# A four-layer graph network on one core: own-group scores in layer 2 formed once and transposed, and both halves of 20 rows in one block in layer 1

## The chip, the cores and the metric

The kernel runs on one core of one Trainium2 chip. The metric is the device time of one execution in microseconds (us). The core has a matrix engine (TensorE, PE in the profile; its weight loads are PEld), a vector engine (VectorE, DVE), an engine for functions of one argument (ScalarE, ACT), a general engine (GpSimd, POOL), an engine that mostly issues transfers (SyncE, SP), and DMA engines that move data between memory (HBM) and the on-chip buffer. TensorE writes its products to a small accumulator memory, PSUM, cut into banks (`BANK = 512` fp32 columns in the code).

## The reference

Four graph layers run one after the other on the same features `x` (2708 x 512) and the same 0/1 adjacency matrix `adj` (2708 x 2708, about 1.2% ones, with ones on the diagonal). Each layer is wrapped in a residual and a normalisation, `x = layernorm(x + layer(x))`. Layers 1 and 2 are the ones the change touches:

```python
def layer1(x, adj, W, b):
    A = (adj != 0).astype(x.dtype)
    hidden = x @ W + b
    deg = jnp.sum(A, axis=0)
    return A @ hidden / deg[:, None]

def layer2(x, adj, weight, bias, node_w, edge_w):
    node_att = softmax(x @ node_w, axis=0)
    h = x @ edge_w
    e = h @ h.T                       # symmetric, 2708 x 2708
    e = jnp.where(adj > 0, e, NEG_BIG)
    edge_att = softmax(e, axis=1)
    support = x @ weight
    return adj * (node_att * edge_att) @ support + bias
```

Layer 0 is a two-pass attention with batch norms and small MLPs, layer 3 a plain attention with `adj` added twice to its scores. Everything is in fp32.

## The kernel before

The 2708 nodes are cut into `NT = 22` blocks: 21 of 128 rows and a last one of `REST = 20`. The 512 features are `C = 4` chunks of 128. The program is written as a sequence of tile operations; a planner decides the order of the instructions on each engine from the order of the program and from its own estimate of when each operand is ready, and it places the semaphores. So work of neighbouring steps is interleaved on an engine, and no order is written out by hand. Each engine then executes its own list in order. Transfers issued by SP (loads) and by POOL (stores and small moves) have a queue each.

**Layer 1** (lines 859 to 967). `hidden` is formed block by block and split into two tiles of the reduced format fp32r, `hid_hi` (rounded) and `hid_lo` (the rest), so that two single-pass products together keep the precision (lines 909 to 915). Both tiles have 22 blocks; the rows 20 to 127 of the last one are zeroed at the start by two DVE memsets (lines 867 and 868). The neighbour sum (lines 924 to 958) takes the rows of the output in groups of four blocks, six groups in all (the last has two). For each block `jt` of keys, SP loads the matching part of the transposed adjacency into `raw` (five buffers), DVE turns it into 0/1 in `at` (three buffers), and PE multiplies it, for each of the group's blocks, with `hid_hi[:, jt, :]` and then `hid_lo[:, jt, :]`, adding up in one PSUM bank per output block. For the last `jt`, `raw` is zeroed first and only 20 rows are loaded.

**Layers 2 and 3** share one function, `softmax_layer` (line 1022). Queries go in seven groups (`GROUPS`) of three blocks, 384 columns; the last group has a fourth block of 20, 404 columns. Layer 2 runs from about 1697 us of the span to 2400. For each group and each of the 22 blocks of keys, `one_score` (line 1086) forms a 128 x 384 block of scores in one of two PSUM banks (`ps_s`), masks it with the adjacency (`masked`: an ACT instruction on the loaded `a_cols`, then a DVE instruction that reads the bank), and takes the running maximum on DVE. When a group is through, `spread_max` (line 1138) turns the column maxima. 25 steps behind the scores, `one_sum` (line 1174) subtracts the maximum (DVE), takes the exponential (ACT), adds to the row sums and multiplies by the adjacency (DVE), and multiplies with the values on PE (line 1195). So the scores of one group run together with the sums of the group before it; in the first group there are only scores, and after the last only sums.

In layer 2 the scores are symmetric, and the kernel uses that between groups (`mirror=True`): a block whose keys belong to a later group is copied from its bank by ACT into `s_raw` (three buffers, tag `sraw`), stored by POOL (lines 1123 to 1126), and later loaded back by SP (`load_kept`) and transposed by PE into the bank (lines 1092 to 1098) in place of being formed again. Blocks whose keys lie in the group itself are formed in full (lines 1099 to 1107): four fp32 matmuls over the chunks of features, each of the full width of the group. `key_order` (line 1031) spreads the blocks that are loaded back evenly among the others. In groups 0 to 4 the three own blocks are among the first of those that are formed, so they stand near the start of the group; in groups 5 and 6 they are spread more widely.

An fp32 matmul is two instructions in the profile, an fp32r matmul or a transposition one.

Of the kernel before, what the change touches and what calls it, by code (L numbers as in the profile page):

```python
# [8 lines left out]
F32 = mybir.dt.float32  # L9
# [8 lines left out]
P = 128  # L18
# [11 lines left out]
def gnn_stack_kernel(  # L30
# [25 lines left out]
    nc = tc.nc  # L56
# [3 lines left out]
    NT = (N + P - 1) // P  # L60
    NFULL = N // P
# [4 lines left out]
    Q = 32  # L66
    REST = N - NFULL * P
# [6 lines left out]
    ident = const.tile([P, P], F32, name="ident")  # L74
# [81 lines left out]
    with ExitStack() as l0:  # L156
# [326 lines left out]
        with (  # L483
# [82 lines left out]
            half = C // 2  # L566
            raws = []
            for name, w in (("wq", wq), ("wk", wk)):
                for part in range(2):
                    tag = "z" if len(raws) == 3 else "a"  # L570
# [21 lines left out]
        with (  # L592
# [18 lines left out]
            for c in range(C):  # L611
                ps = psum.tile([P, F], F32, tag="misc", name="ps_m", bufs=2)
                for o in range(C):
# [5 lines left out]
                        stop=(o == C - 1),  # L619
# [9 lines left out]
            for ci, (c0, w) in enumerate(CHUNKS):  # L629
                pss = []  # L630
                for o in range(C):
# [3 lines left out]
                    ps = pair[:, o % HP, :]  # L635
                    for c in range(C):
# [5 lines left out]
                            stop=(c == C - 1),  # L642
# [12 lines left out]
                for o in range(C):  # L655
                    dst = ft[:, o, c0 : c0 + w]
                    r = elu(
                        att, pss[o][:, :w], w, bias[:, 0, o : o + 1], bias[:, 1, o : o + 1]
                    )
# [4 lines left out]
                while turned < NT and sum(BLOCKS[turned]) <= c0 + w:  # L664
                    j0, n = BLOCKS[turned]
# [193 lines left out]
    with (  # L859
        tc.tile_pool(name="l1", bufs=1) as p1,  # L860
        tc.tile_pool(name="l1ps", bufs=2, space=PSUM) as psum,
        ExitStack() as main,
    ):
        hid_hi = p1.tile([P, NT, F], F32R, name="hid_hi")
        hid_lo = p1.tile([P, NT, F], F32R, name="hid_lo")
        if NFULL < NT:
            nc.vector.memset(hid_hi[:, NFULL, :].bitcast(F32), 0.0)
            nc.vector.memset(hid_lo[:, NFULL, :].bitcast(F32), 0.0)

        work = main.enter_context(tc.tile_pool(name="l1w", bufs=2))
        with tc.tile_pool(name="l1a", bufs=1) as pre:
            b1_sb = load_row(pre, b1, "b1_sb")
            w1_sb = pre.tile([P, C, F], F32, name="w1_sb")
            nc.vector.tensor_copy(w1_sb, w1_held)
            for ci in range(len(early), NCH):
                load_x(ci)
            turned = 0  # L880
            for ci, (c0, w) in enumerate(CHUNKS):
                for c in range(C):
                    cols = ot[:, c, c0 : c0 + w]
                    nc.scalar.activation(
                        cols,
                        cols,
                        AF.Identity,
                        bias=shift3[:, c : c + 1],
                        scale=scale3[:, c : c + 1],
                    )  # L890
                    nc.vector.tensor_tensor(cols, cols, x_held[ci][:, c, :], ALU.add)
                while turned < NT and sum(BLOCKS[turned]) <= c0 + w:
                    it = turned
                    i0, n = BLOCKS[it]
                    tp = psum.tile([P, C, P], F32, tag="po0", name="tp_out")
                    for c in range(C):
                        nc.tensor.transpose(tp[:n, c, :], ot[:, c, i0 : i0 + n], ident)
                    ps = psum.tile([P, F], F32, tag="po1", name="ps_hid")
                    project_rows(ps, ot[:, :, i0 : i0 + n], w1_sb, n)
                    rows = tp[:n].rearrange("p c d -> p (c d)")  # L900
                    mean, rstd = row_stats(rows, n)
                    less = small.tile([P, 1], F32, tag="less", name="less")
                    nc.vector.tensor_scalar(less[:n], mean, rstd, -1.0, ALU.mult, ALU.mult)
                    nc.scalar.activation(xs[:n, it, :], rows, AF.Identity, bias=less[:n], scale=rstd)
                    full = pre.tile([P, F], F32, tag="full", name="full")
                    nc.vector.scalar_tensor_tensor(
                        full[:n], ps[:n], rstd, b1_sb[:n], ALU.mult, ALU.add
                    )
                    nc.scalar.copy(hid_hi[:n, it, :], full[:n])
                    nc.vector.tensor_tensor(  # L910
                        hid_lo[:n, it, :],
                        full[:n],
                        hid_hi[:n, it, :].bitcast(F32),
                        ALU.subtract,
                    )
                    turned += 1

        feats.close()
        l2_weights = ExitStack()
        pw2 = l2_weights.enter_context(tc.tile_pool(name="l2wt", bufs=1, side="right"))  # L920

        G = 4
        later = []
        for g in range(0, NT, G):
            group = range(g, min(g + G, NT))
            c0 = g * P
            w = min(N, c0 + G * P) - c0
            if g == G:
                ew_sb = load_weight(pw2, edge_w, "ew_sb")
                w2_sb = load_weight(pw2, w2, "w2_sb")  # L930
                nw_sb = load_row(pw2, node_w, "nw_sb")
                b2_sb = load_row(pw2, b2, "b2_sb")
            pos = {
                it: psum.tile([P, F], F32, tag=f"po{it - g}", name="ps_nb", bufs=1 + (it - g < 2))
                for it in group
            }
            for jt, (j0, m) in enumerate(BLOCKS):
                if later and jt % 4 == 3:
                    y, n = later.pop(0)
                    layer_norm(y, y, n)  # L940
                raw = work.tile([P, G * P], F32, tag="raw", name="raw", bufs=5)
                a = work.tile([P, G * P], F32R, tag="at", name="at", bufs=3)
                if m < P or w < len(group) * P:
                    nc.vector.memset(raw[:, : len(group) * P], 0.0)
                nc.sync.dma_start(raw[:m, :w], adjT[j0 : j0 + m, c0 : c0 + w])
                nc.vector.tensor_scalar(  # L946
                    a[:, : len(group) * P], raw[:, : len(group) * P], 0.0, None, ALU.not_equal
                )
                for it in group:
                    at = a[:, (it - g) * P : (it - g + 1) * P]  # L950
                    for k, half in enumerate((hid_hi, hid_lo)):
                        nc.tensor.matmul(  # L952
                            pos[it],
                            at,
                            half[:, jt, :],
                            start=(jt == 0 and k == 0),
                            stop=(jt == NT - 1 and k == 1),
                        )
            for it in group:
                n = BLOCKS[it][1]  # L960
                y = xs[:n, it, :]
                nc.vector.scalar_tensor_tensor(
                    y, pos[it][:n], rdeg[:n, it : it + 1], y, ALU.mult, ALU.add
                )
                later.append((y, n))
        for y, n in later:
            layer_norm(y, y, n)
# [5 lines left out]
    GROUP = 3  # L973
    lonely = NT % GROUP == 1
    GROUPS = [list(range(g, min(g + GROUP, NT))) for g in range(0, NT - lonely, GROUP)]
# [46 lines left out]
    def softmax_layer(keys, values, query, score, weigh, finish, after=None, mirror=False):  # L1022
# [6 lines left out]
        HOME = {it: gi for gi, group in enumerate(GROUPS) for it in group}  # L1029
# [17 lines left out]
        with (  # L1047
# [38 lines left out]
            def one_score(st, k):  # L1086
                gi, jt = st["gi"], st["order"][k]
                c0, w = GSPAN[gi]
# [3 lines left out]
                if mirror and HOME[jt] < gi:  # L1092
                    s = load_kept(gi, jt)
                    for b, it in enumerate(GROUPS[gi]):
                        n = BLOCKS[it][1]
                        nc.tensor.transpose(
                            ps[:, b * P : b * P + n], s[:n, b, :], ident[:n, :n]
                        )
                elif m == P:
                    for c in range(C):  # L1100
                        nc.tensor.matmul(  # L1101
                            ps[:, :w],
                            keys[:, c, j0 : j0 + P],
                            st["q"][:, c, :],
                            start=(c == 0),
                            stop=(c == C - 1),
                        )
                else:

                    parts = psum.tile([P, BANK], F32, tag="tp", name="ps_parts")  # L1110
                    for c in range(C):
                        nc.tensor.matmul(
                            parts[c * Q : (c + 1) * Q, :w],
                            keys[:, c, j0 : j0 + Q],
                            st["q"][:, c, :],
                            start=True,
                            stop=True,
                        )
# [401 lines left out]
```

## Time and profile before

| What | Value |
|---|---|
| Median of 3 runs | 3355.96 us (3355.28 to 3361.55) |
| Profiled execution, its own time | 3363.59 us |
| Span of the profiled execution | 3361.8 us |
| Mean granted TensorE clock | 0.985 |
| PE busy | 3272.6 us, 97% of the span |
| DVE / ACT / POOL busy | 1991.5 / 1344.1 / 130.0 us |
| Layer 1's neighbour sum | 1315 to 1536 us |
| Layer 2's attention | 1697 to 2400 us |

A row of the costliest groups reads: line, engine, operation, output and inputs by the program's names, partitions by elements, the number of instructions; then the busy time of all of them together and the mean duration of one in ns; then how long the engine stood idle just before them and what ended most of that. Matmuls overlap, so the busy time of a group is less than number times mean. A row of the busy times by stretch has, after its length, the busy time and the number of instructions of PE, PEld, DVE, ACT and POOL, then the granted clock, the mean share of the DMA engines and their GB/s. A row in order of time has the start, the length, the engine and the instructions merged into it, and in brackets the idle time ahead and what ended it. A row of the waits has who waited for whom, the total in us, how often, and the longest.

### The profile page before, as it was taken

The page shows a single profiled execution, that of the slowest core. Times are in us where ns is not written, and L with a number is a line of the kernel's source. Part 1 is how long each engine was busy: PE and PEld are TensorE (multiplying, and loading weights), DVE is VectorE, ACT ScalarE, POOL GpSimd, SP SyncE. Part 2 cuts the span into 40 slices and gives each one's busy share as a digit, 9 for nine tenths or more (in the row PEclk, how much of TensorE's full clock was granted, in tenths as well). Part 3 has the DMA queues.
Part 4 walks back from the last instruction along what each step waited for, and adds up shares of the span by engine and source line. Part 5 has one row for each costly group of instructions (what it writes and reads, how often), then busy time and mean ns, then how long its engine had stood idle before and what let it go on. Part 6 is the DMA issues. An engine that isn't in the chain of part 4 may idle for free.

```text
span 3361.8 us, 30553 instructions
## 1 busy us (share of the span) xinstructions
PE 3272.6 (97%) x10981; PEld 1751.3 (52%) x10981; DVE 1991.5 (59%) x3228; ACT 1344.1 (40%) x1504; POOL 130.0 (4%) x211
## 2 busy tenths in 40 slices
PE   8999999999999989999999999999999999999998
PEld 5444444544444445886554554444455555555554
DVE  7878967767687585445135666777253442543533
ACT  6888887468877652001133333332011010110110
POOL 1000100000000000000010000000000000000001
PEclk9999999999999999999999999999999999999999
DMA  8746753335534412540044444554211111111100
GB/s 292 249 159 199 274 185 104 112 106 181 183 131 159 157 40 75 140 128 15 0 119 131 118 123 130 141 149 109 63 49 35 44 33 42 37 34 44 35 23 20
DMA packets 168348, 367.32 MB, mean 109 GB/s; under 512 B 20782, under 2 KB 111602, under 8 KB 164804
## 3 DMA queue, kind: packets, MB, share of 16 engines
q1 hardware_dynamic: 153268, 301.55, 30.0%
q0 software_dynamic: 14928, 63.82, 5.0%
q8 instruction: 86, 1.41, 0.2%
q14 instruction: 66, 0.54, 0.1%
HBM read 301.46 MB, written 63.35 MB: 109 GB/s over the span
## 4 chain that ended last, share of the span: by engine, by line
PE 73%; issue 13%; DVE 7%; DMA 3%; ACT 3%; POOL 1%; SPq 0%; POOLq 0%; DVEq 0%; ACTq 0%
PE po L1195 22%; PE ps_s L1101 17%; PE po L397 8%; PE ps_nb L952 7%; PE ps_wide L1013 4%; DVE t L349 3%; PE ps_hid L118 2%; PE ps_sup L1338 2%; PE ps_o L1273 2%; PE ps_mlp L637 2%; DMA a<-adj_d 1%; ACT t L341 1%; DMA a_cols<-in_adjT_dram 1%; PE ps_dec L733 1%; ACT t L350 1%
## 5 line engine op out<-in xcount | busy, mean ns | idle before, releaser
L349 DVE SCALAR_TENSOR_TENSOR t<-t,a 128x2708 f32<-128x2708 f32 (+1 forms) x162 | 480.0, 2974 | 146.6 <-ACT t L341 144.8
L341 ACT ACTIVATE t<-f1b,f2h 128x1354 f32<-128x1354 f32 (+1 forms) x324 | 445.7, 1414 | 93.2 <-PE psm L420 45.1
L397 PE MATMUL po<-t,emb 128*128 128x452 f32 (+3 forms) x1056 | 408.3, 556 | 17.9 <-ACT t L350 10.1
L350 ACT ACTIVATE t<-t 128x2708 f32<-128x2708 f32 (+1 forms) x162 | 396.7, 2452 | 70.3 <-DVE t L349 68.9
L397 PE MATMUL po<-t,xw 128*128 128x452 f32 (+3 forms) x1056 | 415.8, 557 | 9.0 <-ACT ft L499 4.8
L1195 PE MATMUL po<-sup,e 128*128 128x512 f32 x882 | 409.3, 600 | 5.5 <-DVE e L1382 5.5
L1195 PE MATMUL po<-e,xs 128*128 128x384 f32 (+1 forms) x1176 | 407.5, 489 | 0.0
L1101 PE MATMUL ps_s<-q,hT 128*128 128x384 f32 (+1 forms) x1176 | 403.5, 489 | 0.0
L1436 DVE SCALAR_TENSOR_TENSOR e<-a_cols,ps_s 128x384 f32<-128x384 f32 (+1 forms) x154 | 85.6, 556 | 417.3 <-PE ps_s L1101 394.2
L397 PEld LDWEIGHTS po<-t,emb 128*128 128x128 f32 (+1 forms) x1056 | 197.2, 194 | 222.3 <-issue 197.3
L1101 PEld LDWEIGHTS ps_s<-q,hT 128*128 128x128 f32 x1176 | 222.7, 190 | 161.4 <-issue 6.5
L397 PEld LDWEIGHTS po<-t,xw 128*128 128x128 f32 (+1 forms) x1056 | 191.0, 192 | 221.0 <-issue 202.5
L1195 PEld LDWEIGHTS po<-e,xs 128*128 128x128 f32 x1176 | 221.7, 190 | 157.1 <-issue 6.0
L1195 PEld LDWEIGHTS po<-sup,e 128*128 128x128 f32 x882 | 161.8, 191 | 176.5 <-issue 148.4
L1101 PE MATMUL ps_s<-hT 128*128 128x384 f32 (+1 forms) x672 | 229.2, 488 | 1.0 <-ACT sup L1345 0.7
L98 ACT ACTIVATE ln_rstd<-ln_rstd 128x1 f32<-128x1 f32 x88 | 17.2, 201 | 497.5 <-DVE ln_rstd L97 497.0
L1378 ACT ACTIVATE a_cols<-a_cols,neg_big 128x384 f32<-128x384 f32 (+1 forms) x154 | 94.8, 616 | 251.6 <-DMA a_cols<-in_adjT_dram 222.9
L952 PE MATMUL ps_nb<-hid_hi,at 128*128 128x512 f32 x484 | 188.2, 390 | 0.4 <-DVE at L946 0.4
L952 PE MATMUL ps_nb<-hid_lo,at 128*128 128x512 f32 x484 | 187.9, 390 | 0.0
L1172 ACT COPY nmax<-pb 128x384 f32<-128x384 f32 (+1 forms) x14 | 6.7, 478 | 431.2 <-PE pb L1159 350.4
L1101 PEld LDWEIGHTS ps_s<-hT 128*128 128x128 f32 x672 | 125.9, 190 | 97.0 <-issue 19.0
L1190 DVE TENSOR_TENSOR acc<-acc,e 128x384 f32<-128x384 f32 (+2 forms) x294 | 162.6, 553 | 11.2 <-ACT e L1180 1.0
(234 smaller groups left out, 3486.0 us busy)
## 6 DMA issues: line engine op xcount, KB each, us to landing
a<-adj_d SPq DMA_DIRECT2D x116, 677.0 KB
a_cols<-in_adjT_dram SPq DMA_DIRECT2D x378, 192.0 KB
a<-in_adjT_dram SPq DMA_DIRECT2D x42, 677.0 KB
adj_d<-a POOLq DMA_DIRECT2D x42, 677.0 KB, 4.7
raw<-in_adjT_dram SPq DMA_DIRECT2D x105, 256.0 KB
kept<-t POOLq DMA_DIRECT2D x10, 1354.0 KB, 6.4
t<-kept SPq DMA_DIRECT2D x10, 1354.0 KB
a_cols<-in_adjT_dram SPq DMA_DIRECT2D x63, 202.0 KB
```

Source lines behind the costliest of these rows:

```text
L118: nc.tensor.matmul(ps[:n], xt[:, c, :n], w[:, c, :], start=(c == 0), stop=(c == C - 1))
L341: nc.scalar.activation(tv[:, k, :], f1b[:n, k, :w], AF.Tanh, bias=f2h[:n, jt, h : h + 1], scale=0.5,)
L349: nc.vector.scalar_tensor_tensor(tv, tv, GUARD, ab, ALU.add, ALU.mult)
L350: nc.scalar.activation(tv, tv, AF.Exp, scale=0.5)
L397: nc.tensor.matmul(po[HB * k + q][:, :qw], values[r : r + n, jt, h * P : (h + 1) * P], t[r : r + n, k, q0 : q0 + qw], start=(jt == 0), sto ...
L952: nc.tensor.matmul(pos[it], at, half[:, jt, :], start=(jt == 0 and k == 0), stop=(jt == NT - 1 and k == 1),)
L1013: nc.tensor.matmul(ps[:, :width], w(c, o), xt(c), start=(c == 0), stop=(c == C - 1),)
L1101: nc.tensor.matmul(ps[:, :w], keys[:, c, j0 : j0 + P], st["q"][:, c, :], start=(c == 0), stop=(c == C - 1),)
L1190: nc.vector.tensor_tensor(acc, acc, e[:m], ALU.add)
L1195: nc.tensor.matmul(out, lhsT, rhs, start=(k == 0), stop=(k == NT - 1))
L1378: nc.scalar.activation(a, a, AF.Identity, bias=neg_big[: a.shape[0]], scale=1.0e30)
L1436: nc.vector.scalar_tensor_tensor(e, a, 2.0, ps, ALU.mult, ALU.add)
```

## The change

In layer 1 the last block's low half (20 rows) is copied, by one DMA issued by POOL, into rows 32 to 51 of the last block of `hid_hi`. The 20 rows of the adjacency are loaded twice, to rows 0 and 32 of `raw`. For the last block of keys, one product with `hid_hi` then adds both halves, and the product with `hid_lo` is left out. Only the last block of `hid_hi` is zeroed at the start.

In layer 2, of a group's own blocks of keys, the b-th (from 0) is formed only from the group's b-th block of queries on. The parts to the left of it are transposed from copies of earlier own blocks: after own block 0, ACT copies the parts for the second and third blocks (256 columns) from the bank into `s_own`, and after own block 1 the part for the third (128 columns). Own block 1 takes one transposition, own block 2 two. `s_own` shares the three buffers of `s_raw`. In layer 3 nothing changes (`own` is false there).

```diff
         hid_lo = p1.tile([P, NT, F], F32R, name="hid_lo")
-        if NFULL < NT:
-            nc.vector.memset(hid_hi[:, NFULL, :].bitcast(F32), 0.0)
-            nc.vector.memset(hid_lo[:, NFULL, :].bitcast(F32), 0.0)
+
+        nc.vector.memset(hid_hi[:, NT - 1, :].bitcast(F32), 0.0)
...
                     turned += 1
+            nc.gpsimd.dma_start(hid_hi[Q : Q + REST, NT - 1, :], hid_lo[:REST, NT - 1, :])
...
-                nc.sync.dma_start(raw[:m, :w], adjT[j0 : j0 + m, c0 : c0 + w])
+                for r in range(0, P if m == P else 2 * Q, P if m == P else Q):
+                    nc.sync.dma_start(raw[r : r + m, :w], adjT[j0 : j0 + m, c0 : c0 + w])
...
+                halves = (hid_hi, hid_lo) if m == P else (hid_hi,)
                 for it in group:
                     at = a[:, (it - g) * P : (it - g + 1) * P]
-                    for k, half in enumerate((hid_hi, hid_lo)):
+                    for k, half in enumerate(halves):
                         nc.tensor.matmul(
                             pos[it],
                             at,
                             half[:, jt, :],
                             start=(jt == 0 and k == 0),
-                            stop=(jt == NT - 1 and k == 1),
+                            stop=(jt == NT - 1),
                         )
...
                 elif m == P:
+
+                    own = mirror and HOME[jt] == gi
+                    b = jt - GROUPS[gi][0] if own else 0
                     for c in range(C):
                         nc.tensor.matmul(
-                            ps[:, :w],
+                            ps[:, b * P : w],
                             keys[:, c, j0 : j0 + P],
-                            st["q"][:, c, :],
+                            st["q"][:, c, b * P :],
                             start=(c == 0),
                             stop=(c == C - 1),
                         )
+                    for o in range(b):
+                        nc.tensor.transpose(
+                            ps[:, o * P : (o + 1) * P],
+                            st["own"][o][:, (b - o - 1) * P : (b - o) * P],
+                            ident,
+                        )
+                    after_own = (GROUP - b - 1) * P if own else 0
+                    if after_own:
+                        s = att.tile([P, GROUP * P], F32, tag="sraw", name="s_own", bufs=3)
+                        nc.scalar.copy(
+                            s[:, :after_own], ps[:, (b + 1) * P : (b + 1) * P + after_own]
+                        )
+                        st.setdefault("own", []).append(s)
```

## The prediction

> **What bounds the kernel now.** I read the page's busy times and costliest groups first, to see which engine owns the two stages touched.
>
> ```profile
> PE 3272.6 (97%) x10981; PEld 1751.3 (52%) x10981; DVE 1991.5 (59%) x3228; ACT 1344.1 (40%) x1504; POOL 130.0 (4%) x211
> ...
> L1101 PE MATMUL ps_s<-hT 128*128 128x384 f32 (+1 forms) x672 | 229.2, 488 | 1.0 <-ACT sup L1345 0.7
> L952 PE MATMUL ps_nb<-hid_lo,at 128*128 128x512 f32 x484 | 187.9, 390 | 0.0
> ```
>
> TensorE (PE) is the busy engine, and both rows that the change shortens have next to no idle time ahead of them. The mean (488, 390 ns) is not the price of one, since matmuls overlap; the price is the distance from start to start. Next the busy time by stretch: layer 1's neighbour sum, then layer 2 cut where each group's maximum is spread (1760, 1857, ...).
>
> ```profile
> core 0: us, PE busy (x) PEld busy (x) DVE busy (x) ACT busy (x) POOL busy (x), PEclk, DMA share, GB/s
> 1315.00:1536.00 221.00, 220.27 (x968) 181.41 (x968) 99.32 (x280) 4.24 (x21) 0.00 (x0) 1.00 0.50 136
> 1697.00:1760.00 63.00, 61.55 (x197) 35.61 (x198) 26.49 (x51) 25.12 (x47) 12.53 (x23) 1.00 0.53 156
> 1760.00:1857.00 97.00, 96.70 (x277) 48.76 (x276) 56.70 (x117) 31.59 (x62) 8.62 (x16) 1.00 0.43 123
> ...
> 2140.00:2224.00 84.00, 82.19 (x261) 40.55 (x261) 61.93 (x142) 30.18 (x58) 2.15 (x4) 1.00 0.51 147
> 2224.00:2309.00 85.00, 81.87 (x258) 39.56 (x259) 62.47 (x140) 27.05 (x50) 0.00 (x0) 0.98 0.50 138
> ```
>
> In every stretch PE is busy 96% to 100%; over the seven layer 2 stretches up to 2309 it is idle about 8 us of 612. DVE, ACT and the DMA engines stay at or below 75%, 40% and 53%. So a microsecond of PE work removed here should be a microsecond of time, until another engine or the loads become late. What makes PE wait in 1697 to 2309:
>
> ```profile
> PE ps_s L1096 <- DVE e L1379: 1.9, 1, 1.9
> PE po L1195 <- DVE e L1382: 1.6, 4, 0.7
> PE ps_s L1122 <- ACT e L1121: 1.3, 2, 1.0
> ```
>
> These are the largest three. The third matters: it is the one place where PE already waits for an ACT copy of its own product. Last, the instructions in order of time, for the prices.
>
> ```profile
> 27.17 2.95 PE L245 MATMUL pxw<-held,xT_sb 128*128 128x130 f32 x24
> ...
> 1792.47 2.74 PE L1101 MATMUL ps_s<-hT 128*128 128x384 f32 x8
> ...
> 1795.06 2.74 PE L1195 MATMUL po<-sup,e 128*128 128x512 f32 x6
> 1795.30 0.48 ACT L1125 COPY s_raw<-ps_s 128x384 f32<-128x384 f32 x1 [1.12 <-PE ps_s L1101]
> 1795.81 0.55 DVE L1379 SCALAR_TENSOR_TENSOR e<-a_cols,ps_s 128x384 f32<-128x384 f32 x1 [0.33 <-ACT s_raw L1125]
> ...
> 1797.63 0.49 PE L1096 MATMUL ps_s<-ident,s_kept 128*128 128x128 f32 x3
> 1797.96 2.31 PE L1195 MATMUL po<-sup,e 128*128 128x512 f32 x5
> ```
>
> A whole block of scores is eight instructions of 384 columns, two for each of the four chunks of features; from 1792.47 to the next PE work at 1795.06 that is 2.59 us, 0.324 each. Three transposes take 1797.96 - 1797.63 = 0.33, 0.11 each. Twenty-four products of 130 columns, each with its own full weight load, take 2.95 less one latency of about 0.27, over 23 steps: 0.116 each.
>
> **What the Trainium skill says.** FP8 and Floating Point Precision, "TensorE Precision Notes": true FP32 takes four passes through the array. The trace agrees in effect: 384 columns cost 2.59/4 = 0.65 us a matmul, in two records. TensorE: Matmul & The Clock Gate, "Back-to-back issue gap": at the full clock the gap grows with the columns, N/2.4 ns plus little. Four passes of 384 by that are an estimate of 0.65 us, as the trace has it; so narrower scores should pay by column. The same page, "Part 4: PE-mode transpose": about 275 ns for a transpose in a kernel; the trace has a median of 273 ns as the duration but 110 as the pitch, and the pitch is what is paid. PSUM — Partial Sum Buffer, "PSUM bank collisions raise a hardware error": two engines may not touch one bank's same partitions at once, reads included; the trace agrees in that DVE's masking waited 44 times (50.6 us in all) for ACT's copy out of the same bank. The new copies therefore also stand ahead of the masking.
>
> **Part 1, layer 1.** It removes the hid_lo product of the last block: one instruction for each of 22 row blocks. The chain has this sum as 206.42 us for 908 instructions, 0.2273 each; 22 x 0.2273 = 5.0 us, all in a stretch where PE is 99.7% busy. Added: one POOL DMA of 20 rows from hid_lo to hid_hi. It can start after the last hid_lo is written (1317.1 in the trace) and is first needed at block 21 of the first group, 21 x 8 x 0.2273 = 38 us after 1315. POOL's stores of 192 KB in this kernel land in 1.7 to 4.4 us, and its queue is empty here; hidden, and about 4 us at worst if the 38 us of cover were gone. One more load of 20 rows on SP for each of six groups (0.33 us of issue each): five raw buffers run ahead, and DVE waited 94 times for PE in this sum (116.3 us), so the loads are early; nothing. The memset of hid_lo (0.48 us, 1223.63 to the next DVE start at 1224.04) stands in a DVE stretch busy 4.68 of 5 us, while PE waits for the first normalised block: 0.4 us gained, or 0 if the planner puts another ready instruction there. Sum: 5.4 us.
>
> **Part 2, layer 2, what is saved.** Of a group's three own blocks of keys, the second is formed for 128 columns fewer and the third for 256 fewer: together 384 columns, eight instructions, one whole block: 2.59 us. The last group, 404 wide, also loses 384. The third block's narrow products (128, or 148 in the last group) may cost 0.116 by the 130-column row rather than 0.108 by the column rate: 8 x 0.008 = 0.06. Added on PE: 0 + 1 + 2 transposes, 3 x 0.11 = 0.33. Net 2.20 a group, 15.4 for seven.
>
> **Part 2, what may wait.** Two new ACT copies a group, of 256 and 128 columns. The row at hand is 0.48 us for 384; with 0.57 for 512 (the ACT copy into hT) that is about 0.8 ns a column, an estimate of 0.37 and 0.27 us. ACT has 60% idle, so the 14 x 0.32 = 4.5 us of work are free; what costs is lateness. A transposition cannot begin before its copy is done. PE covers that with the narrower scores: 1.73 us (8 x 0.216) for the second block, 0.93 for the third. A copy on an idle ACT is done 0.16 (tail of the last matmul) + 0.12 (two signals) + 0.37 = 0.65 us after the first block, or 0.55 after the second; with one masking of `a_cols` (0.61) ahead of it, 1.26 and 1.16. So the second block's transposition is covered, and the third's may be 0.2 late in group 0, where no other PE work is to be had; later groups have sums (2.58 us a step) to put between. Behind a waiting transposition all of PE is queued: the sums, and the next scores. The bounds: no wait at all from below; from above, the nearest row is the quarters product, which waits for an ACT copy with little cover: 10.3 us over 14 such products in layers 2 and 3, of which 1.3 over seven in layer 2. That is 0.19 a wait here and (10.3 - 1.3)/7 = 1.29 in layer 3. I take 0.19 x 14 = 2.7 us, because layer 2 has the cover; the ends are 0 and 18. The score banks, two of them, are held longer, for transposition, copy and masking; in group 0 the fourth block needs the second's bank about 1.15 us after it is filled, with 0.93 + 0.22 of PE work in between: even. Own blocks write nothing to memory; the three copy buffers shared with `s_raw` hold two own copies and one store. Net of layer 2: 15.4 - 2.7 = 12.7.
>
> **Sum.** 5.4 + 12.7 = 18.1 us. The profiled execution took 3363.6 (span 3361.8 and 1.8 around it), so it would be 3345.5. It stands 7.6 above the median of 3355.96, which I take as run-to-run level that the change leaves alone: 3337.9.
>
> **Rivals.** *Late copies* (the one that ends slower). ACT runs in order, and at the start of groups 1 to 4, just where the own blocks stand, it has runs of exponentials: five in 2.18 us, six would be 2.9. A copy behind such a run comes 2.9 + 0.65 - 1.73 = 1.8 late for the second block and 2.9 + 0.55 - 0.93 = 2.5 for the third: 4.3 in each of six groups, 26 us against a gain of 20.8: about 3361. It breaks even at 1.5 us a wait and is measurably slower from 2.0. For it: the order of ACT is fixed ahead of time by a planner, and layer 3's 1.29. Against: copies of `s_raw` amid the same exponentials came 0.1 to 0.6 us after their matmuls. *Other limits take over in the last three groups.* DVE is 74% busy there and waits for `a_cols` loads; if their gain is lost, 3 x 2.2 = 6.6 less: about 3344.5. Against: PE still idles only 3% there. *Narrow products don't pay by column.* A weight load lasts 190 ns; if the third block is paced by it, 8 x 0.075 = 0.6 a group, 4.2 in all: about 3342. Against: the 130-column row, with the same load, ran at 0.116. *The change does less than it says*: excluded, as the widths are in the slices.
>
> **How the numbers follow.** About 0.2% (6.7 us) is what a measurement of this kernel can tell from no change. A gain of 14 to 24 us, the forecast and its near variants with narrow products: 0.62. A gain of 7 to 14 (last groups limited, or waits near 0.7 each): 0.19. Within 6.7 (waits near 1.3, or a poorer interleaving at the group starts): 0.10. Slower: 0.09. Faster thus 0.81. The range starts at the full gain without any wait (20.8) and some 3 us of run spread, 3332, and reaches over the second case, to 3349.
>
> **What would show it.** Right: 462 hid_lo products instead of 484; 21 new transpositions; the neighbour sum 5 us shorter; own blocks two and three in 1.8 to 1.9 and 1.1 to 1.2 us of PE; the maxima of groups spread about 2 us closer together each. Wrong: a row in which PE waits for the new ACT copy for over 10 us in all, PE idle well above 8 us between the layer's start and the last spread maximum, or `a_cols` loads ending PE's waits.

## The result and the profile after

The changed kernel takes 3347.91 us in the median (3343.16 to 3352.47, 8 runs) against 3359.05 (3355.28 to 3363.02, 8 runs) for the kernel before: a ratio of 0.9965 with a 95% interval of 0.9956 to 0.9974. That is 11.8 us less, 8.7 to 14.8. The forecast of 3338 us with 18.1 us of gain had the sign and the range right, and the mechanism in the stages that the change touches; a third of the gain is missing. The profiled execution has a span of 3342.5 us, 19.3 below that of before, but 7.7 of these lie ahead of layer 1's sum, where the change touches next to nothing; there TensorE ran at half clock for 55 us in this execution and for 75 in that of before.

The rows of the page that answer to those shown of before:

```profile
PE 3251.5 (97%) x10980; PEld 1741.6 (52%) x10980; DVE 1988.9 (60%) x3227; ACT 1347.6 (40%) x1518; POOL 130.7 (4%) x212
...
L1106 PE MATMUL ps_s<-hT 128*128 128x384 f32 (+5 forms) x672 | 212.3, 461 | 2.4 <-DVE e L1397 1.7
L954 PE MATMUL ps_nb<-hid_lo,at 128*128 128x512 f32 x462 | 179.9, 389 | 0.0
```

The scores of layer 2 have the same 672 instructions, now in narrower forms and 16.9 us less busy; 22 products with `hid_lo` are gone. ACT has 14 instructions more, the copies, and POOL one, the transfer. The busy time by stretch, with the cuts where the maxima are now spread:

```profile
core 0: us, PE busy (x) PEld busy (x) DVE busy (x) ACT busy (x) POOL busy (x), PEclk, DMA share, GB/s
1307.00:1524.00 217.00, 215.88 (x947) 176.99 (x946) 98.15 (x279) 4.56 (x22) 0.51 (x1) 1.00 0.52 140
1686.00:1747.00 61.00, 58.84 (x200) 35.12 (x200) 26.23 (x51) 25.42 (x50) 12.53 (x23) 1.00 0.53 157
1747.00:1842.00 95.00, 95.00 (x280) 48.26 (x279) 56.23 (x117) 31.11 (x63) 8.61 (x16) 1.00 0.45 128
...
2202.00:2285.00 83.00, 79.86 (x262) 39.32 (x261) 63.05 (x141) 27.65 (x52) 0.00 (x0) 0.98 0.52 143
2285.00:2390.00 105.00, 94.55 (x274) 42.24 (x274) 48.04 (x125) 25.37 (x47) 4.67 (x6) 0.92 0.24 67
```

Every group is shorter and still bound by PE. The last row, which has no partner among the rows shown before, is the one to look at: the sums of the last group and layer 3's first query, with a granted clock of 0.92. The same work in the kernel before:

```profile
2309.00:2410.00 101.00, 90.42 (x272) 40.35 (x271) 47.82 (x124) 25.28 (x46) 4.67 (x6) 0.95 0.24 70
```

An own second and third block of keys (group 2), in order of time, in the changed kernel:

```profile
1848.07 1.89 PE L1106 MATMUL ps_s<-hT 128*128 128x256 f32 x8
1849.80 0.27 PE L1114 MATMUL ps_s<-ident,s_own 128*128 128x128 f32 x1
1849.91 2.74 PE L1213 MATMUL po<-sup,e 128*128 128x512 f32 x6
...
1853.07 1.14 PE L1106 MATMUL ps_s<-hT 128*128 128x128 f32 x8
1854.05 0.38 PE L1114 MATMUL ps_s<-ident,s_own 128*128 128x128 f32 x2
1854.27 2.10 PE L1106 MATMUL ps_s<-hT 128*128 128x384 f32 x6
```

From start to start the second block takes 1849.91 - 1848.07 = 1.84 us with its transposition, the third 1854.27 - 1853.07 = 1.20 with two: the forecast had 1.73 + 0.11 and 0.93 + 0.22. The 256 columns cost two thirds of 384 and the 128 a little over one third; narrow products do pay by column.

What PE waits for between the first score and the last spread maximum of the changed kernel:

```profile
PE ps_s L1098 <- DVE e L1397: 2.3, 2, 1.9
PE ps_s L1106 <- DVE e L1397: 1.7, 3, 0.9
PE po L1213 <- DVE e L1400: 1.4, 3, 0.7
...
PE ps_s L1114 <- ACT s_own L1122: 0.8, 1, 0.8
```

Of twenty-one transpositions one waited for a copy, 0.8 us. The second row was 0.3 us in the kernel before; the 1.4 more fit the bank that is now held longer.

Cut into stages at the first and the last product of the neighbour sum, the first score of layer 2, the last spread maximum of layer 2 and the first score of layer 3, the two first profiles and the runs that follow read, in us:

| Kernel | to layer 1's sum | the sum | up to layer 2's scores | seven groups | last sums | layer 3 |
|---|---|---|---|---|---|---|
| before | 1314.9 | 220.4 | 162.2 | 611.5 | 101.2 | 951.6 |
| before, again | 1309.8 | 220.4 | 162.2 | 611.1 | 101.4 | 951.6 |
| changed | 1307.2 | 216.5 | 162.5 | 599.2 | 104.2 | 952.9 |
| changed, again | 1313.1 | 216.5 | 162.4 | 599.6 | 104.0 | 952.9 |
| layer 1 alone | 1314.5 | 216.4 | 162.4 | 611.5 | 101.4 | 951.6 |
| layer 2 alone | 1311.3 | 220.3 | 162.2 | 599.3 | 103.9 | 953.0 |
| changed + 1.7 | 1310.7 | 216.5 | 164.3 | 598.5 | 103.2 | 952.9 |
| changed + 3.4 | 1311.1 | 216.4 | 166.0 | 598.8 | 104.6 | 951.3 |
| before + 1.7 | 1317.9 | 220.4 | 164.0 | 610.0 | 104.8 | 951.3 |
| changed, filled | 1312.6 | 216.6 | 162.4 | 599.6 | 99.0 | 949.9 |
| before, filled | 1313.1 | 220.4 | 162.1 | 610.8 | 99.1 | 951.3 |
| no copies | 1311.5 | 216.5 | 162.5 | 598.3 | 104.9 | 951.6 |
| less VectorE | 1310.9 | 215.9 | 162.4 | 599.7 | 104.4 | 952.9 |
| three fills | 1310.3 | 215.9 | 162.5 | 598.3 | 99.0 | 951.6 |

The first column differs by up to 10 us between executions; the others repeat within 0.5 us where the kernel is the same. So the table shows what a difference of medians can't. In means over three traces each (the single edits counted where they agree with one of the two kernels) the sum gained 3.9 us and the groups 12.0; the edit of layer 1 lost 0.2 again right behind the sum; and 2.7 + 1.3 = 4.0 were lost in two stages that the change leaves as they were. 3.9 + 12.0 - 0.2 - 4.0 = 11.7, against 11.8 by the ratio and 11.1 by the medians.

### The profile page after: what moved, and what is told of

It is laid out like the page before. It is cut to its first block, busy times and chain, and to the rows that moved or that the text cites. A ratio compares the mean times of both kernels' runs of the same rounds, so it can differ in the third digit from the quotient of the medians.

```text
span 3342.5 us, 30573 instructions
## 1 busy us (share of the span) xinstructions
PE 3251.5 (97%) x10980; PEld 1741.6 (52%) x10980; DVE 1988.9 (60%) x3227; ACT 1347.6 (40%) x1518; POOL 130.7 (4%) x212
## 4 chain that ended last, share of the span: by engine, by line
PE 72%; issue 13%; DVE 9%; DMA 3%; ACT 3%; POOL 1%; SPq 0%; POOLq 0%; DVEq 0%; ACTq 0%
PE po L1213 21%; PE ps_s L1106 17%; PE po L397 9%; PE ps_nb L954 6%; PE ps_wide L1015 4%; DVE t L349 3%; PE ps_hid L118 2%; PE ps_sup L1356 2%; PE ps_o L1291 2%; PE ps_mlp L637 1%; DMA a<-adj_d 1%; PE ps_dec L733 1%; ACT t L341 1%; DMA a_cols<-in_adjT_dram 1%; ACT t L350 1%
## 5 line engine op out<-in xcount | busy, mean ns | idle before, releaser
L1106 PE MATMUL ps_s<-hT 128*128 128x384 f32 (+5 forms) x672 | 212.3, 461 | 2.4 <-DVE e L1397 1.7
L954 PE MATMUL ps_nb<-hid_lo,at 128*128 128x512 f32 x462 | 179.9, 389 | 0.0
L1208 DVE TENSOR_TENSOR acc<-acc,e 128x384 f32<-128x384 f32 (+2 forms) x294 | 162.5, 553 | 12.2 <-ACT e L1198 2.3
```

Of the source, the lines that this page charges most:

```text
L954: nc.tensor.matmul(pos[it], at, half[:, jt, :], start=(jt == 0 and k == 0), stop=(jt == NT - 1),)
L1106: nc.tensor.matmul(ps[:, b * P : w], keys[:, c, j0 : j0 + P], st["q"][:, c, b * P :], start=(c == 0), stop=(c == C - 1),)
L1208: nc.vector.tensor_tensor(acc, acc, e[:m], ALU.add)
```

## The experiments

### Each part alone, and both kernels again

The question was whether what is missing comes each time or was an accident of one execution. For the 4.0 us behind the groups theory A is the accident and theory B says each time; for the sum of layer 1 the letters stand the other way about. A half-clock window, in these forecasts, is a stretch of 3.41 us in which TensorE ran at half its clock; the next section shows them. The edit of layer 1 alone is the first part of the diff above, with the old scores:

```diff
+            nc.gpsimd.dma_start(hid_hi[Q : Q + REST, NT - 1, :], hid_lo[:REST, NT - 1, :])
...
-                    for k, half in enumerate((hid_hi, hid_lo)):
+                    for k, half in enumerate(halves):
```

> The edit of layer 1 alone, layer 2 as before. Prediction: 5.4 us faster (5.0 of TensorE work, 0.4 of memset). Theory A (what the trace of the changed kernel shows of the stage holds): the neighbour sum 3.6 us shorter than 220.25 us, not 5.0, because TensorE waits for VectorE about 1.4 us more where the sixth group begins. Theory B (the shortfall was an accident of that execution): 5.0 us shorter.

Measured: 3356.45 us against 3359.94 for before (ratio 0.9992, 0.9984 to 1.0000). The sum took 216.4 us, 3.9 to 4.0 less and not 5.0; layer 2 and 3 are as before. Theory A's 3.6 was near, theory B's 5.0 is out: the shortfall in layer 1 is lasting.

The edit of layer 2 alone is the second part, with the old layer 1:

```diff
-                            ps[:, :w],
+                            ps[:, b * P : w],
...
+                    for o in range(b):
+                        nc.tensor.transpose(
```

> The edit of layer 2 alone, layer 1 as before. Prediction: 12.7 us faster. Theory A (the gain is made in the groups and kept; the rest is half-clock windows that fall differently from run to run): from the first score to the last spread maximum 12 to 13 us shorter than 611.5 us, and the whole kernel 12 to 13 us faster within its interval. Theory B (the shorter groups shift what follows into more half-clock windows each time): the same 12 to 13 us in the groups, but the last sums and layer 3's first group 3 to 4 us longer again, and the whole kernel only 8 to 9 us faster.

Measured: 3352.97 us (ratio 0.9974, 0.9963 to 0.9985), 8.7 us less. The groups are 599.3 us, the last sums 103.9 and layer 3 953.0. That is theory B, in size and in place: the groups gain 12.0 and the stages behind them lose 4.0, and it is the edit of layer 2 that does it.

The changed kernel once more, no edit:

> The changed kernel as it is, for a second profiled execution and more times. Theory A: layer 1's sum and the seven groups of layer 2 have the same lengths as in the first profile within 0.2 us (216.6 and 599.2 us), while layer 0, the last sums of layer 2 and layer 3 differ by some us as half-clock windows fall; the median gain nears 16 us. Theory B: the last sums and layer 3 are again some 4 us longer than before, and the gain stays at 11 to 12 us.

Measured: 3349.45 us (ratio 0.9962, 0.9950 to 0.9975), with 104.0 and 952.9 us again. And the kernel before once more, no edit:

> The kernel before as it is, for a second profiled execution and as the measure of the comparison: 0 us. Both theories: layer 1's sum 220.25 us and the groups of layer 2 611.5 us within 0.2 us. Theory A: layer 0, the last sums of layer 2 and layer 3 differ from the first profile by several us through half-clock windows alone, with the same program.

Measured: 3361.42 us (ratio 0.9999, 0.9991 to 1.0007); 101.4 and 951.6 us, the same as in its first profile, while the stages ahead of the sum are 5.1 us shorter. For the stages behind the groups theory A is out: the loss comes each time.

### Where the 4 us are

The last sums have the same instructions in both kernels, in the same order as far as their long runs go, and wait for the same two things, 3.9 us soon after their start and 6.2 us at the end of the layer. Call these the two idle spots. What differs is how fast PE runs after such a wait. The changed kernel, then the kernel before, the first twelve sums after the first wait, and the query of layer 3 after the second:

```profile
2297.19 8.06 PE L1213 MATMUL po<-sup,e 128*128 128x512 f32 x12 [3.93 <-DVE e L1400]
...
2377.33 12.41 PE L1015 MATMUL ps_wide<-hT,mqk 128*128 128x384 f32 x32 [0.32 <-ACT hT L1008]
```

```profile
2320.89 6.84 PE L1195 MATMUL po<-sup,e 128*128 128x512 f32 x12 [3.93 <-DVE e L1382]
...
2399.76 10.59 PE L1013 MATMUL ps_wide<-hT,mqk 128*128 128x384 f32 x32 [0.45 <-ACT hT L1006]
```

Same instructions, same idle time ahead, 1.2 and 1.8 us longer. The weight loads of the changed kernel show why; each goes with one PE instruction of 512 columns:

```profile
2300.77 0.34 PEld L1213 LDWEIGHTS po<-sup,e 128*128 128x128 f32 x1 [0.52 <-issue]
2301.62 0.34 PEld L1213 LDWEIGHTS po<-sup,e 128*128 128x128 f32 x1 [0.52 <-DVE e L1400]
2302.47 0.23 PEld L1213 LDWEIGHTS po<-sup,e 128*128 128x128 f32 x1 [0.52 <-issue]
2302.94 0.19 PEld L1213 LDWEIGHTS po<-sup,e 128*128 128x128 f32 x1 [0.24 <-issue]
2303.37 0.19 PEld L1213 LDWEIGHTS po<-sup,e 128*128 128x128 f32 x1 [0.24 <-issue]
```

They come 0.85 us apart until 2302.5 and 0.43 after: TensorE runs at half its clock for the first 5.4 us of work after the wait. The granted clock of the same stretches says so (changed kernel, then before):

```profile
2297.20:2302.60 5.40, 5.40 (x7) 2.30 (x8) 5.40 (x17) 1.67 (x3) 0.00 (x0) 0.51 0.45 115
2303.00:2306.00 3.00, 3.00 (x13) 1.51 (x14) 3.00 (x9) 0.82 (x2) 0.00 (x0) 1.00 0.46 133
```

```profile
2320.90:2323.60 2.70, 2.70 (x3) 1.16 (x4) 2.70 (x8) 0.20 (x1) 0.00 (x0) 0.50 0.38 87
2324.00:2330.00 6.00, 6.00 (x21) 2.63 (x20) 6.00 (x18) 3.17 (x5) 0.00 (x0) 1.00 0.53 135
```

In the kernel before, the work after the same wait ran slowly for 2.9 us, until 2323.8. Each such stretch costs half its length: 2.7 against 1.45 here, and the difference is the 1.2 us of the rows above. In all fourteen traces the half-clock stretches (but for the one that runs on past the kernel's end) last a whole number of 3.41 us and start on a grid of that period within each execution. The Trainium skill (TensorE: Matmul & The Clock Gate, "What's actually happening") describes this: the clock is halved after an idle window of about 3.4 us and restored after a busy one, and the windows run on their own; the traces agree in the two states (0.50 and 1.00) and in the period. They differ in one thing: the idle window need not be idle throughout. In the changed kernel TensorE stopped at 2293.3 us and the clock was halved at 2295.7, after 2.4 us.

So the grid theory: where an idle spot of a given length falls on the grid decides how many slow windows follow it. After the layer 2 edit the two spots fall elsewhere than before, and one more window follows each; a third one more comes early in layer 3. Its rival was that the planner's new order of instructions costs the time.

### Moving the idle spots

The changed kernel with more work ahead of layer 2's groups, the first block's products formed once more for 256 columns and written over:

```diff
+                    if mirror and gi == 0 and k == 0:
+                        for _ in range(1):
+                            for c in range(C):
+                                nc.tensor.matmul(
+                                    ps[:, :256],
+                                    keys[:, c, j0 : j0 + P],
+                                    st["q"][:, c, :256],
+                                    start=(c == 0),
+                                    stop=(c == C - 1),
+                                )
```

> The changed kernel with 1.72 us more TensorE work ahead of layer 2's first block (its four products formed once more for 256 columns and overwritten; results the same). Grid theory (half-clock windows of 3.41 us lie on a fixed grid, and the idle spots of TensorE at the end of layer 2 now fall at a worse place in it): the groups 1.7 us longer, but the last sums back from 104.0 to about 101.4 us and layer 3 from 952.9 to 951.6, so the whole about 2 us faster than the changed kernel. Structure theory (the new order of the instructions itself costs the 4 us): last sums and layer 3 stay, the whole 1.7 us slower than the changed kernel.

Measured: 3347.66 us (ratio 0.9964, 0.9952 to 0.9977). The first slow stretch fell back to one window, the second stayed at three: last sums 103.2 us instead of the expected 101.4, layer 3 unchanged. The forecast of the grid theory was only half met: the second spot stayed as the structure theory had it. 0.7 us of the added work was also hidden in the first group. The same, twice over:

```diff
+                    if mirror and gi == 0 and k == 0:
+                        for _ in range(2):
```

> The changed kernel with 3.44 us more TensorE work at the same place, which is one whole period of the grid. Grid theory: last sums 104.0 and layer 3 952.9 us as in the changed kernel, the whole 3.4 us slower than it. Structure theory: the same.

Measured: 3348.40 us (ratio 0.9958, 0.9946 to 0.9971). The last sums are 104.6 us, as expected near the 104.0 of the changed kernel, but layer 3 has one window less, 951.3; so the 3.4 us of added work are not seen in the whole. It doesn't decide between the theories, since both forecast the same, and both missed. By the trace the first group grew by 2.1 us only, so the spots did not move by the whole period that was meant. The first edit put into the kernel before:

```diff
                 elif m == P:
+                    if mirror and gi == 0 and k == 0:
+                        for _ in range(1):
+                            for c in range(C):
...
                     for c in range(C):
```

> The kernel before with 1.72 us more TensorE work at the same place. Grid theory: the idle spots move from the good to the bad place, so the last sums go from 101.4 to about 104 us and layer 3 from 951.6 to 952.9, and the whole is 5 to 6 us slower than before. Structure theory: the whole is 1.7 us slower, last sums and layer 3 unchanged.

Measured: 3364.89 us (ratio 1.0011, 1.0003 to 1.0019), slower by 3.7 us by the ratio (1.0 to 6.4) and 4.8 by the medians. The times alone would leave room for the structure theory's 1.7; the stages don't. The last sums went from 101.2 to 104.8 us, with not one instruction of them changed, and their clock fell from 0.95 to 0.92:

```profile
2312.00:2417.00 105.00, 94.55 (x272) 42.06 (x271) 47.94 (x125) 25.03 (x46) 4.68 (x6) 0.92 0.23 68
```

Of the added work only 0.3 to 0.7 us shows in scores and groups together. Layer 3 did not lengthen as the theory had it. The main point is shown: the old kernel gets the loss in the last sums when its idle spots move; the new order of instructions isn't needed for it. Which place on the grid gives how many windows was forecast less well, one spot right out of two in the first run.

Read afterwards from the eleven traces in which the two spots are not filled, the place does decide. Start of the idle spot, in us after the last line of the grid:

| Idle spot | Fewer slow windows | More slow windows |
|---|---|---|
| 3.9 us, start of the last sums | one window: 2.2 to 3.4 (4 traces) | two windows: 0.2 to 1.4 (7 traces) |
| 6.2 us, end of layer 2 | two windows: 1.0 to 1.2 (3 traces) | three windows: 3.0 to 3.4 and 0.1 to 0.2 (8 traces) |

No trace falls out of line, in either kernel. The changed kernel with 1.7 us more has its first spot on the good side (2.2) and its second still on the bad one (0.2): the half that was met and the half that wasn't.

### Filling the idle spots

If idle spots are the cause, work in them that keeps TensorE busy should take the windows away. Ten products with the identity, not used, placed after the sums of the last but one group (four) and of the last (six); the planner put five into each spot:

```diff
                         end(states.pop(gi))
+                        if mirror and gi + 2 >= len(GROUPS):
+                            fill = psum.tile([P, BANK], F32, tag="ps_s", name="fill")
+                            for _ in range(4 if gi + 2 == len(GROUPS) else 6):
+                                nc.tensor.matmul(
+                                    fill, ident, values[:, 0, :], start=True, stop=True
+                                )
```

> The changed kernel with ten products of the identity with a block of values (0.86 us each, their result not used) put into the two idle spots of TensorE at the end of layer 2, five in each. Grid theory: the half-clock windows at 2307, 2382 and 2460 us go or become fewer, the last sums fall from 104.0 to 97 to 101 us, layer 3 to 951 to 952, the whole 4 to 7 us faster than the changed kernel. If the windows have another cause than the idle spots: no change, or up to 1 us slower.

(The times of windows named in this and a later expectation count from another zero, about 11 us before the span's.) Measured: 3341.91 us (ratio 0.9939, 0.9926 to 0.9951), 18.2 us below before and 7.5 below the second measurement of the changed kernel (7.7 by the ratios). The stretch of the last sums, with 8.6 us of work more in it, is 5 us shorter, at full clock:

```profile
2286.00:2385.00 99.00, 96.90 (x292) 41.63 (x291) 50.71 (x132) 24.04 (x44) 2.02 (x4) 1.00 0.23 64
```

The fills in order of time, with the sums and the query that follow them:

```profile
2298.96 4.54 PE L1326 MATMUL fill<-sup,ident 128*128 128x512 f32 x10
2303.34 3.17 PE L1213 MATMUL po<-sup,e 128*128 128x512 f32 x7
...
2371.83 3.70 PE L1326 MATMUL fill<-sup,ident 128*128 128x512 f32 x8
...
2379.75 10.59 PE L1015 MATMUL ps_wide<-hT,mqk 128*128 128x384 f32 x32 [0.45 <-ACT hT L1008]
```

Layer 3 also fell, to 949.9 us, with no slow window left at its start; in the version with all of it, below, the same fills leave one there. In size this is a little more than the grid theory's forecast of 4 to 7 us. The same fill in the kernel before:

> The kernel before with the same two fills at the end of layer 2 as in the filled changed kernel. Grid theory: the last sums fall from 101.4 to 99 us and layer 3 from 951.6 to 950 us, 4 us in all, so that it takes about 3356; against it the filled changed kernel (3341.9) is then 14 to 16 us faster, the 3.9 + 12.0 us that the change saves in its own two stages. If the change has a lasting cost behind its stages, the distance stays at 11 to 12 us.

Measured: 3357.61 us (ratio 0.9991, 0.9983 to 0.9999), with last sums of 99.1 us, again at full clock. With both kernels filled, the distance is 3357.61 - 3341.91 = 15.7 us, and by the ratios 0.9991 - 0.9939 = 0.0052, 17.5 us (by their two intervals some 12 to 22). By stages it is 3.8 us in the sum, 11.2 in the groups, nothing in the last sums, and 1.4 in layer 3, where a slow window is left in the kernel before alone. So the change is worth 15 to 16 us in its own two stages, and the loss behind them is the clock's: with the idle spots filled it is gone, with no lasting cost in its place.

### The price of the copies

The copies and the wait for them taken away, by transposing parts of the keys, which are there long before:

```diff
-                            st["own"][o][:, (b - o - 1) * P : (b - o) * P],
+                            keys[:, o, j0 : j0 + P],
...
-                    after_own = (GROUP - b - 1) * P if own else 0
-                    if after_own:
-                        s = att.tile([P, GROUP * P], F32, tag="sraw", name="s_own", bufs=3)
```

> The changed kernel without the fourteen copies of own scores: the 21 new transpositions turn parts of the keys instead, which are there long before, so the scores left of an own block are those of another matrix; the number, size and place of TensorE's instructions stay. It prices what the copies and the wait for them cost. Prediction: 2.7 us of waits. Late-copy rival: 10 us and more. From the trace of the changed kernel (0.8 us of waiting for the copy, 1.7 us for the bank that is held longer): the seven groups 599.3 us become 597 to 598.5.

Measured: the groups took 598.3 us instead of 599.3 (3343.07 us, ratio 0.9951, 0.9937 to 0.9964, from four runs that spread over 7 us; its windows fell differently, so the whole says little). The first group alone fell from 61.1 to 59.5 us, the next five changed by 0.6 at most; the last had one slow window more (83.9 against 82.9), so the price is 1 to 2 us. That is within what was taken (2.7), and far from the rival's 10 and more. It also leaves 1.4 to 2.4 us of the 3.4 between the 15.4 us saved on paper and the 12.0 measured that the copies don't explain; where these are was not found.

### Layer 1's missing microsecond

In the sum, PE waits for VectorE where the sixth group begins:

```profile
PE ps_nb L954 <- DVE at L947: 1.1, 2, 0.6
```

In the kernel before it is 0.4. VectorE has there to empty four banks (2.73 us), to normalise, and to zero `raw` before each load, since the sixth group is only 148 wide. With less of that:

```diff
-                if m < P or w < len(group) * P:
-                    nc.vector.memset(raw[:, : len(group) * P], 0.0)
+                if m < P:
+                    nc.vector.memset(raw[:, :w], 0.0)
...
-                    a[:, : len(group) * P], raw[:, : len(group) * P], 0.0, None, ALU.not_equal
+                    a[:, :w], raw[:, :w], 0.0, None, ALU.not_equal
...
-                            pos[it],
+                            pos[it][:n],
```

> The changed kernel with less VectorE work in layer 1's sixth group: no memset of raw except for the last block of keys, 148 columns compared instead of 256, and the products with the last block of rows take 20 columns. If VectorE's evacuation of the fifth group and these memsets are what kept 1.4 of the 5.0 us (theory A of the first runs): layer 1's sum falls from 216.5 to 215.2 to 215.6 us. If the shortfall lies elsewhere: it stays at 216.5 us. The whole changes by 1 us at most, less than can be told from times.

Measured: the sum took 215.9 us (216.5 before this edit; the whole 3348.00 us, ratio 0.9967, 0.9952 to 0.9982, no difference that can be told), and the wait is 0.4 us again. Half met: taking VectorE's work away gives back 0.6 of the 1.1 us that the layer 1 edit fell short of 5.0. The kernel before has these memsets too and was not run without them, so the share is an indication. The traces place the rest: summed over the starts of PE's products, 1.0 us arises where the sixth group begins, where PE waits for VectorE, and 0.1 where the four groups ahead of it begin. And this edit pays some of its gain back: in its sixth group the products start 0.233 us apart instead of 0.227, about 0.4 us in all.

### A version with all of it

```diff
+            fill = psum.tile([P, BANK], F32, tag="misc", name="fill", bufs=2)
+            for _ in range(28):
+                nc.tensor.matmul(fill[:, :P], ones, ident, start=True, stop=True)
```

These stand between layer 0 and layer 1, together with the two fills of layer 2 and the last edit of layer 1.

> A version meant to beat both: the changed kernel with the idle spots at the end of layer 2 filled, less VectorE work in layer 1's sixth group, and 28 small products of ones with the identity (results not used) in the 7 us in which TensorE waits between layer 0 and layer 1. Grid theory: also the windows at 1231 us go; from the first idle-spot fill's 3341.9 us another 2 to 3 us less, about 3339.

Measured: 3339.44 us (ratio 0.9940, 0.9928 to 0.9953), 21 us below before. It can't be told apart from the two fills alone (0.9939). The slow windows between the two layers are gone from its trace, but one came back in layer 3 (951.6 us).

## Why the prediction was right or wrong

*What bounds the kernel.* Right. PE stayed the bound in each stretch, and most of the saved PE work turned into time in its own stage.

*The prices by column, and the transpositions.* Right, to 0.05 us a block (1.84 and 1.20 us against 1.84 and 1.15).

*Layer 1's 5.4 us.* Mis-sized: 3.9 us in the sum. The 22 products went, but "nothing" for what VectorE does at the start of the sixth group was wrong by about 1.0 us, of which an experiment took 0.6 away. Behind the sum another 0.2 went. The 0.4 us of the memset can't be seen: the stage ahead of the sum varies by 10 us from execution to execution.

*Layer 2's 12.7 us.* Measured 12.0 (611.3 to 599.3). The waits that came, 2.2 us by the profile and 1 to 2 by the run without copies, are of the size taken, but not where it was put: one wait of 0.8 us for a copy instead of fourteen of 0.19, and some 1.4 that fit the bank held longer, which the text had called even. The near hit of the whole has luck in it. The upper end of 18 us and the 1.29 us a wait in layer 3 rest on a misreading: the 10.3 us count 8.4 us in which weight loads stood idle, beside running products. PE itself waited 1.9 us, 1.3 of it in layer 2.

*The sum.* This is the step that cost most of the missing third: it ended with the stages it touched, and took for granted that work behind them keeps its length. That "a microsecond of PE work removed here should be a microsecond of time" holds only while what follows runs at the same clock. The last sums and layer 3 became 4.0 us longer through slow windows after two idle spots, shown by moving the spots in the old kernel and by filling them in both. 18.1 - 1.5 (layer 1) - 0.2 (behind it) - 0.7 (layer 2) - 4.0 (clock) = 11.7.

*The level.* That the profiled execution's distance from the median is a matter of the execution was right, and the traces show where such differences sit: ahead of layer 1's sum, with 51 to 75 us of half clock by execution. But the median of three runs, 3355.96, was itself low by chance: with eight it is 3359.05. Of the 10.0 us between 3337.9 forecast and 3347.9 measured 3.1 are that.

*The rivals.* Late copies: out (0.8 us waited; 1 to 2 us in all). Its row of exponentials was read too short (five in 2.18 us make 2.6 for six, not 2.9, and the trace has eight in 3.80), but nothing came to wait behind them. The last three groups limited by something else: out, they gained 1.6, 2.3 and 2.2 us between the first profiles. Narrow products paced by the weight load: out. The case that came, a gain of 7 to 14 us, had a chance of 0.19, for causes that were not the real one.

## What to carry to other kernels

Shortening work on the bounding engine moves every idle spot behind it, and where TensorE's clock drops after idle spots, the same spot can cost a slow window more or less by where it falls; compare the lengths and the granted clock of the stages that were not touched before crediting or blaming the edit. A short idle spot of TensorE on the path can be worth filling with products that nobody uses: here 8.6 us of them made the kernel 7.5 us faster. Compare two versions once more with such spots filled before taking a loss behind the edit for its price. Against run-to-run noise of 5 us, stage lengths that repeat within 0.5 us tell what medians can't.

## What was not expected of the hardware

An idle time of 3.9 us left TensorE at half clock for 2.9 to 3.4 or for 4.9 to 6.1 us of the following work, by its place in a grid of 3.41 us. A shorter one does it too: the single wait of 1.9 us in the last group, the longest that the prediction lists, is followed by one or two slow windows in all fourteen traces. The grid isn't as free of the program as a clock of its own suggests: in thirteen of the fourteen traces the first neighbour sum starts 0.8 to 1.5 us after a line of the grid, and the one exception is the kernel with the idle spot just ahead of it filled. That a slow stretch ends on the grid, and so ties the work after it to the grid, would explain why the 4 us came each time; this was argued, not tried.
